# A transformer block on one core: the first LoRA stage run in attention's tiles by the second one's code, with sequence 0's projections dealt into its last rounds

## The chip, the cores and the metric

The kernel runs on one core of a Trainium2 chip. The metric is the device time of one execution in microseconds (us), as the median of several runs of the same build. The core has five engines that take their instructions in order, each from its own stream: TensorE (PE, matmuls and transposes into PSUM), VectorE (DVE), ScalarE (ACT), GpSimd (POOL) and SyncE (SP, which issues the DMAs).

## The reference, cut to what matters

The input `x` has 16 sequences of 512 positions by 256 features, in float32. Six steps follow each other, each added to the residual stream: an FP4-quantised feed-forward, a Mamba mixer, a second pass of the same feed-forward, a LoRA mixture, attention, and the same LoRA mixture again.

```
x = x + 0.5 * ffn(layernorm(x))        # FP4 weights and activations
x = x + mamba(layernorm(x))
x = x + 0.5 * ffn(layernorm(x))        # the same weights
x = x + 0.5 * lora(layernorm(x))       # the first LoRA stage
x = x + attention(layernorm(x))        # 16 heads of 16, ALiBi, causal
x = x + 0.5 * lora(layernorm(x))       # the second LoRA stage, same weights

lora(x):  base   = x @ base_w.T + base_b            # 256 -> 256
          gate   = softmax(x @ router_w.T + router_b).astype(bf16)   # 8 experts
          mid    = x @ lora_A                       # rank 8
          out    = sum_e gate[e] * (mid @ lora_B[e])
          return base + 2 * out
```

## The kernel before, in words

The residual stream stays in SBUF as sixteen tiles `xs[b]`, each with 128 positions on the partitions, 4 chunks and 256 features. `ffn_phase` (L181) runs twice. The last instruction of its second pass on PE is the matmul of L331, and the last Silu of ACT is that of L291.

**The first LoRA stage** is `lora_phase` (L947) with its own pools: two PSUM tiles of two banks under the tag `ob`, two banks under `tr` and two under `o`. It loops over 19 rounds with a pipeline of four steps. In round b it runs `experts(b-3)`, `base(b-2)`, `turn(b-1)` and `norm(b)`. Of each sequence,

- `norm` takes the statistics on DVE (`bn_stats`, `bn_aggr`, L969 and L970), a square root on ACT (L972), a reciprocal and a product on DVE (L974, L976), and the normalised rows on ACT (L981, four instructions);
- `turn` transposes them on PE (L126, eight transposes) and copies them out on ACT (L129, two copies);
- `base` multiplies by the 272 columns of base weight, router and LoRA A (L1001), takes the sums out on DVE (L1005, L1010), and makes the softmax of the gate and the products `cb` with small DVE instructions and an exponential on ACT (L1013 to L1026);
- `experts` transposes `cb` (L1036), copies it on ACT (L1040), multiplies by the stacked LoRA B (L1045) and adds on DVE (L1050).

Between the rounds it draws steps of `constants` (L1102), a generator that loads attention's weights and fills its constants: the query and key tiles on DVE (L1152, L1157), and the `mx` and `va` tiles on POOL (L1185, L1189). In its last three rounds it also normalises and transposes sequence 0 for attention, and runs that sequence's projections by `heads` (L1251) with plain, unpinned matmuls. There the raw queries and keys are parked in the tiles `vas[1:]`, which are filled with ones only afterwards (L1306).

**Attention** is `attn_phase` (L1084). Its pools are opened after `lora_phase` has closed its own: one of SBUF (`a`), and PSUM with two tiles of two banks under `sp`, one under `sw`, and two banks under `mm`. All its PE instructions go through `matmul` and `transpose` (L1199, L1202), which keep them in the order in which the program gives them. So a trace shows them all under L1200 and L1203. `project(b)` (L1205) is a generator: it normalises sequence b (statistics L1214, a logarithm and an exponential on ACT at L1223 and L1224, two Newton steps on DVE, the rows at L1235), transposes it, and multiplies by the query, key and value weights. Each query or key tile leaves by eight DMAs from SP (L1288). `begin(b)` starts it. A unit is one sequence and four heads: `peak_score` and `peak_max` (masked scores and their row maxima, L1346 and L1350) in six steps, then `peak_rows` (L1355, a transpose of the maxima), then `weigh_score`, `weigh_exp`, `apply` and `divide`. The loop over the units (L1697) deals projections and closing work in between by `aside` (L1483).

**The second LoRA stage** has no pools of its own. It borrows attention's: `parts(b)` (L1519) cuts its small tiles out of free query and key tiles (`free`) and of one exponent tile (`rows_of`), and its PSUM tiles are `mm` and `sp`. `mix_norm` (L1533) takes the statistics on DVE, a logarithm and an exponential on ACT (L1545, L1546), then a chain of ten small POOL instructions (L1548 to L1556, two Newton steps and the shift), then the rows on ACT (L1572). `mix_turn`, `mix_base` and `mix_experts` do what `turn`, `base` and `experts` do. `mix_first` handles sequences 0 and 1 beside attention's last units; `mix_rest` the other fourteen, one round each, in an order that is written out:

```
for of in (
    turn, base, base, expert, turn, base, expert, base, expert
):
```

Every instruction that the program does not pin is placed by a scheduler at build time; on the chip each engine then runs its stream in order.

Of the kernel before, what the change touches and what calls it, by code (L numbers as in the profile page):

```python
# [9 lines left out]
F32 = mybir.dt.float32  # L10
BF16 = mybir.dt.bfloat16
# [5 lines left out]
P = 128  # L17
# [19 lines left out]
def macaron_kernel(  # L37
# [83 lines left out]
    def transpose_seq(xh, dst, psum_pool, tag, order=lambda ins: ins):  # L121

        for k in range(KD):
            pt = psum_pool.tile([P, SEQ], F32, name="pt", tag=tag)
            for c in range(NC4):
                order(nc.tensor.transpose(  # L126
                    pt[:, c * P : (c + 1) * P], xh[:, c, k * P : (k + 1) * P], ident
                ))
            nc.scalar.copy(dst[:, k, :], pt)  # L129

# [50 lines left out]
    def ffn_phase(weights, src, dst, prepare=None, raws=(), keep=()):  # L181
        wgT, wuT, wdT = weights
        HF = DFF // 2
        with tc.tile_pool(name="f", bufs=2) as fp, tc.tile_pool(
# [90 lines left out]
            def make_h(b, pair, j):  # L275
# [3 lines left out]
                for half in range(2):  # L279
# [11 lines left out]
                    nc.scalar.activation(sl, g, AF.Silu)  # L291
# [655 lines left out]
    def lora_phase(weights, last, beside=None, heads=None):  # L947


        wx, lb, br = weights  # L950
        W = D + NE + NR
        with tc.tile_pool(name="l", bufs=2) as lp, tc.tile_pool(
            name="l_b", bufs=2, space=PSUM
        ) as ps_b, tc.tile_pool(name="l_ps", bufs=2, space=PSUM) as ps:
            xhs, xTs, copies = {}, {}, []

            cbs = []
            for i in range(3):
                cb = lp.tile([P, NC4, NX], F32, name=f"cb{i}", tag=f"cb{i}", bufs=1)
                nc.gpsimd.memset(cb[:, :, NE * NR :], 1.0)  # L960
                cbs.append(cb)

            def norm(b):

                x = xs[b]
                st = lp.tile([P, NC4, 6], F32, name="st", tag="st")
                mv = lp.tile([P, NC4, 2], F32, name="mv", tag="mv")
                for c in range(NC4):
                    nc.vector.bn_stats(out=st[:, c, :], in_=x[:, c, :])  # L969
                    nc.vector.bn_aggr(out=mv[:, c, :], in_=st[:, c, :])  # L970
                sd = lp.tile([P, NC4], F32, name="sd", tag="sd")
                nc.scalar.activation(sd, mv[:, :, 1], AF.Sqrt, bias=eps)  # L972
                rs = lp.tile([P, NC4], F32, name="rs", tag="rs")
                nc.vector.reciprocal(rs, sd)  # L974
                nm = lp.tile([P, NC4], F32, name="nm", tag="nm")
                nc.vector.scalar_tensor_tensor(  # L976
                    nm, mv[:, :, 0], -1.0, rs, op0=ALU.mult, op1=ALU.mult
                )
                xh = lp.tile([P, NC4, D], F32, name="xh", tag="xh")
                for c in range(NC4):  # L980
                    nc.scalar.activation(  # L981
                        xh[:, c, :], x[:, c, :], AF.Identity,
                        bias=nm[:, c : c + 1], scale=rs[:, c : c + 1],
                    )
                xhs[b] = xh

            def turn(b):
                xT = lp.tile([P, KD, SEQ], F32, name="xT", tag="xT")
                transpose_seq(xhs.pop(b), xT, ps, "tr")
                xTs[b] = xT  # L990

            def base(b):

                xT = xTs.pop(b)
                s = lp.tile([P, NC4, NE + NR], F32, name="s", tag="s")
                for half in range(2):
                    o = ps_b.tile([P, 2, SEQ], F32, name="ob", tag="ob")
                    for j in range(2):
                        c = 2 * half + j
                        for k in range(KD):  # L1000
                            nc.tensor.matmul(  # L1001
                                o[:, j, :W], lhsT=xT[:, k, c * P : (c + 1) * P],
                                rhs=wx[:, k, :], start=(k == 0), stop=(k == KD - 1),
                            )
                    nc.vector.tensor_tensor(  # L1005
                        s[:, 2 * half : 2 * half + 2, :], o[:, :, D:W],
                        br.unsqueeze(1).to_broadcast([P, 2, NE + NR]), op=ALU.add,
                    )
                    xc = xs[b][:, 2 * half : 2 * half + 2, :]
                    nc.vector.tensor_tensor(xc, xc, o[:, :, :D], op=ALU.add)  # L1010
                lg, mid = s[:, :, :NE], s[:, :, NE:]
                mx = lp.tile([P, NC4], F32, name="mx", tag="mx")
                nc.vector.tensor_reduce(mx, lg, axis=AX.X, op=ALU.max)  # L1013
                ex = lp.tile([P, NC4, NE], F32, name="ex", tag="ex")
                nc.vector.tensor_tensor(
                    ex, lg, mx.unsqueeze(2).to_broadcast([P, NC4, NE]), op=ALU.subtract
                )
                nc.scalar.activation(ex, ex, AF.Exp)
                nc.vector.tensor_reduce(mx, ex, axis=AX.X, op=ALU.add)
                nc.vector.reciprocal(mx, mx)  # L1020
                gt = lp.tile([P, NC4, NE], BF16, name="gt", tag="gt")
                nc.vector.tensor_tensor(
                    gt, ex, mx.unsqueeze(2).to_broadcast([P, NC4, NE]), op=ALU.mult
                )
                cb = cbs[b % 3]
                nc.vector.tensor_tensor(  # L1026
                    cb[:, :, : NE * NR].rearrange("p c (e r) -> p c e r", e=NE),
                    gt.unsqueeze(3).to_broadcast([P, NC4, NE, NR]),
                    mid.unsqueeze(2).to_broadcast([P, NC4, NE, NR]), op=ALU.mult,
                )  # L1030

            def experts(b):
                cb = cbs[b % 3]
                pt = ps.tile([P, SEQ], F32, name="ct", tag="tr")
                for c in range(NC4):
                    nc.tensor.transpose(  # L1036
                        pt[:NX, c * P : (c + 1) * P], cb[:, c, :], ident
                    )
                cT = lp.tile([NX, SEQ], F32, name="cT", tag="cT")
                copies.append(nc.scalar.copy(cT, pt[:NX, :]))  # L1040
                for half in range(2):
                    o = ps.tile([P, 2, D], F32, name="o", tag="o")
                    for j in range(2):
                        c = 2 * half + j
                        nc.tensor.matmul(  # L1045
                            o[:, j, :], lhsT=cT[:, c * P : (c + 1) * P], rhs=lb,
                            start=True, stop=True,
                        )
                    xc = xs[b][:, 2 * half : 2 * half + 2, :]
                    nc.vector.tensor_tensor(xc, xc, o, op=ALU.add)  # L1050
                if last:
                    store_x(b)

            for b in range(NB + 3):
                if 0 <= b - 3:
                    experts(b - 3)
                if 0 <= b - 2 < NB:
                    base(b - 2)
                if 0 <= b - 1 < NB:
                    turn(b - 1)  # L1060
                if b < NB:
                    norm(b)
                if heads is not None:
                    if 0 < b < NB:
                        next(beside, None)
                        if b % 2:
                            next(beside, None)
                    if b == NB - 1:
                        for _ in beside:
                            pass  # L1070
                    if b == NB:
                        norm(0)
                    if b == NB + 1:
                        turn(0)
                        first = heads(0, xTs.pop(0), None, ps, "tr", nc.tensor.matmul)
                        for _ in range(4):
                            next(first)
                    if b == NB + 2:
                        for _ in first:
                            pass  # L1080
        return copies[-1]


    def attn_phase(weights):  # L1084
# [17 lines left out]
        def constants(aw):  # L1102
# [79 lines left out]
            for r in range(3):  # L1182
                if r < 2:
                    mx = aw.tile([P, NC4, 4, 32], F32, name=f"mx{r}")
                    nc.gpsimd.memset(mx, 0.0)  # L1185
                    mxs.append(mx)
                va = aw.tile([P, NC4, VW], F32, name=f"va{r}")
                if r == 0:
                    nc.gpsimd.memset(va, 1.0)  # L1189
                vas.append(va)  # L1190
# [14 lines left out]
        def project(b):  # L1205
# [43 lines left out]
            yield from heads(b, xT, ap, ps, "mm", matmul)  # L1249

        def heads(b, xT, ap, ps, tag, matmul):  # L1251


# [609 lines left out]
```

## Time and profile before

| | |
|---|---|
| median of 3 runs | 4329.45 us (4329.03 to 4329.85) |
| the profiled execution | 4323.53 us, its span 4321.8 us |
| mean granted PE clock | 0.976 of full |
| busy share of the span | PE 92%, DVE 86%, ACT 54%, POOL 39% |
| first matmul of the first LoRA stage to its last projection | 2999.92 to 3140.21 us |
| first attention unit's scores begin | 3140.99 us |

The span is what the profiler records of the execution; the execution's own time lies 1.73 us above it, and the median of the plain runs 5.92 us above the profiled one. A busy share is an average over all stages. What a stage is worth is read from the stretch of time in which it runs: which engine is busy there, and what each idle stretch waited for. Times in a trace are counted from the start of the span.

### The profile page before, as it was taken

What the parts mean: (1) busy time and instruction counts of PE and PEld (TensorE: products, weight loads), DVE (VectorE), ACT (ScalarE), POOL (GpSimd) and SP (SyncE); (2) the same over time, 40 slices, a digit from 0 to 9 for tenths busy, and PEclk for the clock granted to TensorE, in tenths of its full rate; (3) what the DMA queues carried; (4) which work ended last, traced back from release to release, by engine and by line L of the source; (5) the groups of instructions that cost most, each with busy time, mean ns of one, the idle gap of its engine ahead of it and who ended that gap; (6) DMA issues with size and microseconds to landing.
All of it is one profiled execution on the core that took longest, in us unless ns stands there. A gap on an engine that the chain in (4) does not pass through costs nothing. (4 is left out here: it accounts for less than half of the span.)

```text
span 4321.8 us, 51496 instructions
## 1 busy us (share of the span) xinstructions
PE 3980.8 (92%) x18786; PEld 2179.5 (50%) x18786; DVE 3735.6 (86%) x4950; ACT 2315.4 (54%) x3478; POOL 1672.8 (39%) x1102
## 2 busy tenths in 40 slices
PE   6999977989888899888888799998999999999999
PEld 4666632333333333333333466666745555555557
DVE  9999838999999999999999899997678778878776
ACT  4444346676767677677666344434624444444434
POOL 3000027888888888888889400000000000000001
PEclk9999999999999999999999999999989999999999
DMA  4000024344444444444442300000010000000002
GB/s 151 15 15 20 15 109 129 119 137 128 127 132 133 141 142 142 142 142 141 142 139 82 114 1 1 1 1 16 2 24 16 18 19 16 18 20 14 20 11 69
DMA packets 120895, 305.16 MB, mean 71 GB/s; under 512 B 25329, under 2 KB 45362, under 8 KB 104002
## 3 DMA queue, kind: packets, MB, share of 16 engines
q1 hardware_dynamic: 120642, 301.88, 22.3%
q8 instruction: 148, 2.42, 0.2%
q14 instruction: 105, 0.86, 0.1%
HBM read 239.68 MB, written 45.35 MB: 66 GB/s over the span
## 5 line engine op out<-in xcount | busy, mean ns | idle before, releaser
L487 POOL TENSOR_TENSOR bx<-dtu,bc 128x1024 f32<-128x1024 f32 x512 | 1193.6, 2359 | 47.5 <-DVE h L883 47.3
L493 PE MATMUL y<-g,ident 128*128 128x512 f32 x2048 | 1007.3, 630 | 130.3 <-DVE g L490 130.1
L883 DVE TENSOR_TENSOR_SCAN h<-da,bx 128x1024 f32<-128x1024 f32 x384 | 879.7, 2291 | 85.4 <-ACT da L484 48.8
L484 ACT ACTIVATE da<-dt,a_neg 128x511 f32<-128x511 f32 x1024 | 703.0, 688 | 217.7 <-DVE hs L883 117.6
L493 PEld LDWEIGHTS y<-g,ident 128*128 128x128 f32 x2048 | 388.3, 198 | 710.0 <-issue 461.9
L1397 ACT ACTIVATE eT<-s 128x768 f32<-128x768 f32 (+1 forms) x384 | 338.6, 882 | 481.0 <-PE s L1200 481.0
L490 DVE TENSOR_TENSOR g<-h,bc 128x1024 f32<-128x1024 f32 x384 | 468.9, 1221 | 28.6 <-DVE h L883 1.4
L1200 PE MATMUL s<-k,q 32*128 32x256 f32 (+3 forms) x2048 | 479.5, 477 | 5.4 <-DVE mx L1350 4.5
L1350 DVE TENSOR_REDUCE mx<-s 128x2 f32<-128x1024 f32 (+3 forms) x512 | 410.3, 823 | 12.4
L1200 PE MATMUL s<-qm,k 32*128 32x512 f32 (+3 forms) x2048 | 387.1, 473 | 8.9 <-ACT eT L1397 7.7
L1600 POOL MEMSET k<- 128x4 f32 x2 | 0.2, 105 | 950.4 <-DVE ku L1282 946.9
L1346 DVE TENSOR_TENSOR s<-s,mask 128x256 f32<-128x256 f32 (+1 forms) x384 | 199.3, 519 | 194.1 <-PE s L1200 191.2
L487 POOL TENSOR_TENSOR g<-hs,bc 128x1024 f32<-128x1024 f32 x128 | 301.3, 2354 | 157.7 <-DVE hs L883 140.4
L291 ACT ACTIVATE sl<-g 128x352 f32<-128x352 f32 x256 | 118.1, 464 | 384.6 <-PE g L286 381.6
L1200 PEld LDWEIGHTS s<-k,q 32*128 32x128 f32 x2048 | 218.6, 186 | 164.1 <-DVE s L1346 80.5
L883 DVE TENSOR_TENSOR_SCAN hs<-da,bx 128x1024 f32<-128x1024 f32 x128 | 291.9, 2281 | 2.5 <-ACT da L484 2.5
L493 PE MATMUL p<-xT,w_in 128*128 128x512 f32 x500 | 242.2, 607 | 19.7 <-ACT xT L484 10.1
L484 ACT ACT_TABLE_LOAD x170 | 218.1, 1283 | 3.0
L960 POOL MEMSET cb<- 128x4 f32 x3 | 0.2, 104 | 561.4 <-PE o L331 561.4
L1200 PEld LDWEIGHTS s<-qm,k 32*128 32x128 f32 x2048 | 170.8, 186 | 58.7 <-ACT eT L1397 42.0
L516 POOL MEMSET xs<- 128x12 f32 x2 | 0.2, 110 | 512.7 <-DMA xd<-x 512.7
L286 PE MATMUL g<-wgT,xT 128*128 128x352 f32 x512 | 182.4, 466 | 0.0
(311 smaller groups left out, 6925.6 us busy)
## 6 DMA issues: line engine op xcount, KB each, us to landing
bc<-bd SPq DMA_DIRECT2D x128, 1024.0 KB, 6.6
xs<-xc SPq DMA_DIRECT2D x240, 256.0 KB, 4.7
xc<-xp SPq DMA_DIRECT2D x60, 256.0 KB, 2.0
x<-_attn_hidden_states_dram SPq DMA_DIRECT2D x16, 512.0 KB, 7.6
xd<-x SPq DMA_DIRECT2D x16, 512.0 KB, 2.6
xo<-xd SPq DMA_DIRECT2D x16, 512.0 KB, 3.6
xe<-xo SPq DMA_DIRECT2D x16, 512.0 KB, 2.6
x<-xe SPq DMA_DIRECT2D x16, 512.0 KB, 10.2
```

What stands on the lines that cost most here:

```text
L286: nc.tensor.matmul(dst, lhsT=xT[:, k, c * P : (c + 1) * P], rhs=w[:, k, f0 : f0 + HF], start=(k == 0), stop=(k == KD - 1),)
L291: nc.scalar.activation(sl, g, AF.Silu)
L484: return tc.keep_in_program_order(nc.scalar.activation(out, in_, func, **kw))
L487: tc.keep_in_program_order(nc.gpsimd.tensor_tensor(out, in0, in1, op=op))
L490: tc.keep_in_program_order(nc.vector.tensor_tensor(out, in0, in1, op=op))
L493: tc.keep_in_program_order(nc.tensor.matmul(out, **kw))
L516: nc.gpsimd.memset(t[:, :, : DCONV - 1], 0.0)
L883: tc.keep_in_program_order(nc.vector.tensor_tensor_scan(flat(h), flat(das[t % 2]), flat(bxs.pop(t)), 0.0, op0=ALU.mult, op1=ALU.add,))
L1200: tc.keep_in_program_order(nc.tensor.matmul(out, **kw))
L1346: nc.vector.tensor_tensor(own, own, const["mask"][:, :w].unsqueeze(1).to_broadcast([P, 2, w]), op=ALU.add)
L1350: nc.vector.tensor_reduce(mx[:, t, 2 * pair : 2 * pair + 2, RM], s[:, :, off : off + (t + 1) * P], axis=AX.X, op=ALU.max,)
L1397: const["exp"] = nc.scalar.activation(eT[:, 2 * pair : 2 * pair + 2, e0 : e0 + w], s[:, :, :w], AF.Exp)
```

## The change

`lora_phase` goes, with its pools, and so does `heads` as a function of its own: its body is again part of `project`. The second stage's functions serve the first stage too. The list `free` stays empty until attention's last sequence, and the functions ask it which stage they are in. While it is empty, all small tiles come from the two exponent tiles in `rows_of`, the rows are normalised on ACT, and nothing is stored. `mix_rest` becomes `mix_rounds(first)`. In the first stage it also draws one step of `constants` per round, begins sequence 0's normalisation in round 16 (of 1 to 19), and lets its projections run from round 17 on: one step of them follows each step of the LoRA work. The rest of them, and `begin(1)`, follow behind. The `va` tiles are all filled with ones by `constants`. The table of logarithm and exponential is loaded on ACT behind the feed-forward's last Silu.

On each engine the streams before and after are the same up to the end of the second feed-forward, except for that table load. They are the same again, in the same order, from early in attention's first units on; on PE the streams differ from the first LoRA transposes up to the last of sequence 0's value projections.

```diff
+    silu = []
...
-                    nc.scalar.activation(sl, g, AF.Silu)
+                    silu.append(nc.scalar.activation(sl, g, AF.Silu))
...
-    def lora_phase(weights, last, beside=None, heads=None):
...
-            for b in range(NB + 3):
-                if 0 <= b - 3:
-                    experts(b - 3)
-                if 0 <= b - 2 < NB:
-                    base(b - 2)
-                if 0 <= b - 1 < NB:
-                    turn(b - 1)
-                if b < NB:
-                    norm(b)
...
                 va = aw.tile([P, NC4, VW], F32, name=f"va{r}")
-                if r == 0:
-                    nc.gpsimd.memset(va, 1.0)
+                nc.gpsimd.memset(va, 1.0)
...
-            yield from heads(b, xT, ap, ps, "mm", matmul)
-
-        def heads(b, xT, ap, ps, tag, matmul):
...
         with tc.tile_pool(name="aw", bufs=1) as aw:
-            behind = lora_phase(weights, False, constants(aw), heads)
...
-                with tc.issue_after(behind.ins):
+                with tc.issue_after(silu[-1].ins):
                     const["exp"] = nc.scalar.preload_act_table_set("natural_log_exp_and_others")
...
-                begin(1)
...
-                free = [t for j in range(NJ) for t in (qs[at(NB - 2, j)], ks[at(NB - 2, j)])]
+                free = []
...
-                    if b % 4 < 2:
+                    if free and b % 4 < 2:
                         four = free[4 * (b % 2) : 4 * (b % 2) + 4]
                     else:
-                        e = rows_of[0].rearrange("p i w -> p (i w)")
+                        e = rows_of[b % 4 // 2].rearrange("p i w -> p (i w)")
...
-                    if b >= 4:
+                    if b >= 4 or not free:
                         nc.gpsimd.tensor_tensor(g, mv[:, :, 0], rs, op=ALU.mult)
                         nc.gpsimd.tensor_scalar(g, g, -1.0, None, op0=ALU.mult)
...
-                        if b < 4:
+                        if b < 4 and free:
                             nc.vector.tensor_scalar(
...
-                    m = 1 if b < 2 else 2
+                    m = 1 if b < 2 and free else 2
...
-                        if half_ == 1:
+                        if half_ == 1 and free:
                             store_x(b)
...
-                def mix_rest():
+                def mix_rounds(first):
-                    for n in range(3, NB + 4):
+                    for n in range(first + 1, NB + 4):
                         none = iter(())
                         turn = mix_turn(n - 1) if n - 1 < NB else none
-                        base = mix_base(n - 2) if 2 <= n - 2 < NB else none
-                        expert = mix_experts(n - 4) if 2 <= n - 4 else none
-                        if 4 <= n < NB:
+                        base = mix_base(n - 2) if first <= n - 2 < NB else none
+                        expert = mix_experts(n - 4) if first <= n - 4 else none
+                        if first + 2 <= n < NB:
                             mix_norm(n)
+                        if not free:
+                            if n < NB:
+                                next(making, None)
+                            if n == NB:
+                                begin(0)
+                                normed = coming.pop(0)
+                            if n == NB + 1:
+                                coming[0] = normed
                         for of in (
                             turn, base, base, expert, turn, base, expert, base, expert
                         ):
...
+                making = constants(aw)
+                for _ in range(2):
+                    rows_of.append(ap.tile([P, 4, EW], F32, name="eT", tag="eT"))
+                mix_norm(0)
+                mix_norm(1)
+                for _ in mix_rounds(0):
+                    next(coming.get(0, none_left), None)
+                for _ in coming.pop(0):
+                    pass
+                started.clear()
+                begin(1)
...
-                        ahead = coming.pop(A[0] + 1, None) or mix_first()
+                        ahead = coming.pop(A[0] + 1, None)
+                        if ahead is None:
+                            for j in range(NJ):
+                                free.extend((qs[at(NB - 2, j)], ks[at(NB - 2, j)]))
+                            ahead = mix_first()
...
-                            rows_of.append(ap.tile([P, 4, EW], F32, name="eT", tag="eT"))
-                            ahead = itertools.chain(ahead, mix_rest())
+                            rows_of[1] = ap.tile([P, 4, EW], F32, name="eT", tag="eT")
+                            ahead = itertools.chain(ahead, mix_rounds(2))
```

More of the change, by code (lines that the diff above doesn't have):

```diff
@@ L945, in lora_weights @@
         return wx, lb, br
-    def lora_phase(weights, last, beside=None, heads=None):
[L950 to L1052, printed above, removed]
-            for b in range(NB + 3):
-                if 0 <= b - 3:
-                    experts(b - 3)
-                if 0 <= b - 2 < NB:
-                    base(b - 2)
-                if 0 <= b - 1 < NB:
-                    turn(b - 1)
-                if b < NB:
-                    norm(b)
[L1063 to L1081, printed above, removed]
@@ L1248, in project @@
                 yield 2, False
-            yield from heads(b, xT, ap, ps, "mm", matmul)
-        def heads(b, xT, ap, ps, tag, matmul):
-            x = xs[b]
-            spare = iter(())
-            if ap is None:
-                spare = iter(
-                    [
-                        va.rearrange("p c w -> p (c w)")[:, i * SEQ : (i + 1) * SEQ]
-                        for va in vas[1:] for i in range(2)
-                    ]
-                )
             bvb, bob, bq_t, bk_t = (const[n] for n in ("bvb", "bob", "bq_t", "bk_t"))
@@ L1265, in heads @@
                 for name, ring in (("q", qs), ("k", ks)):
-                    p = ps.tile([P, SEQ], F32, name="p", tag=tag)
+                    p = ps.tile([P, SEQ], F32, name="p", tag="mm")
                     for k in range(KD):
@@ L1273, in heads @@
                             yield 3, True
-                    r = next(spare, None)
-                    if r is None:
-                        r = ap.tile([P, SEQ], F32, name=f"{name}u", tag=f"{name}u")
+                    r = ap.tile([P, SEQ], F32, name=f"{name}u", tag=f"{name}u")
                     if name == "q":
@@ L1293, in heads @@
             for half in range(2):
-                p = ps.tile([P, 2, D], F32, name="p", tag=tag)
+                p = ps.tile([P, 2, D], F32, name="p", tag="mm")
                 for c in range(2):
@@ L1303, in heads @@
                         yield 3, True
-                if ap is None and half == 0:
-                    for va in vas[1:]:
-                        nc.gpsimd.memset(va, 1.0)
                 dst = vas[b % 3][:, 2 * half : 2 * half + 2, : NH * HV]
@@ L1465, in attn_phase @@
                 pools.update(sbuf=ap, psum=ps)
-                with tc.issue_after(behind.ins):
+                with tc.issue_after(silu[-1].ins):
                     const["exp"] = nc.scalar.preload_act_table_set("natural_log_exp_and_others")
                 units = [(b, j) for b in range(NB) for j in range(NJ)]
-                coming = {}
+                coming, none_left = {}, iter(())
                 def begin(b):
```

## The prediction

> **What bounds the kernel now.** I read the page's slices first: PE is 0.9 busy through attention, but not where the first LoRA stage lies (about 2994 to 3140 us), and the clock row is full nearly everywhere. So I asked for the stretch of that stage and of the step into attention, in windows.
>
> ```profile
> core 0: us, PE busy (x) PEld busy (x) DVE busy (x) ACT busy (x) POOL busy (x), PEclk, DMA share, GB/s
> ...
> 3010.00:3020.00 10.00, 8.06 (x42) 6.10 (x41) 9.67 (x42) 9.80 (x17) 0.00 (x0) 1.00 0.00 0
> ...
> 3100.00:3110.00 10.00, 9.71 (x50) 8.00 (x49) 5.84 (x17) 4.14 (x9) 0.00 (x0) 1.00 0.00 0
> ...
> 3140.00:3150.00 10.00, 2.79 (x15) 1.34 (x15) 9.74 (x36) 0.41 (x2) 1.06 (x1) 0.75 0.21 48
> 3150.00:3160.00 10.00, 10.00 (x25) 4.11 (x25) 6.73 (x21) 1.86 (x3) 1.06 (x1) 0.50 0.05 10
> ```
>
> Early rounds are bound by DVE and ACT (both near 10 of 10), late ones by PE. Then comes a hole: PE has 2.79 of 10 us of work, and behind it the clock is at half. Windows of 2 us show half clock from 3145 until
>
> ```profile
> 3170.00:3172.00 2.00, 2.00 (x10) 0.63 (x4) 0.90 (x3) 0.54 (x1) 0.00 (x0) 0.50 0.25 53
> 3172.00:3174.00 2.00, 2.00 (x8) 0.73 (x10) 0.86 (x1) 0.78 (x2) 0.00 (x0) 0.94 0.02 5
> ```
>
> The timeline names the hole:
>
> ```profile
> 3136.59 3.62 PE L1298 MATMUL p<-wv,xT 128*128 128x256 f32 x16
> ...
> 3140.99 1.14 PE L1200 MATMUL s<-k,q 32*128 32x512 f32 x8 [0.78 <-DVE va L1308]
> ...
> 3148.55 2.30 PE L1203 MATMUL p<-ident,xh 128*128 128x128 f32 x8 [6.42 <-DVE xh L1235]
> ...
> 3167.12 1.11 PE L1203 MATMUL p<-ident,mx 128*128 128x128 f32 x4
> ```
>
> PE waits for sequence 1's normalised rows, because its statistics start on DVE only at 3141.45. The first unit (3140.21 to 3167.12) takes 26.9 us; later ones take about 16 (o matmuls at 3235.34 and 3251.51).
>
> What the second stage's code costs per round, the same trace shows at its end, by ACT's copies of `cT`:
>
> ```profile
> 4247.19 0.58 ACT L1651 COPY q<-p 65x512 f32<-65x512 f32 x1 [1.56 <-PE p L1203]
> ...
> 4253.90 0.58 ACT L1651 COPY q<-p 65x512 f32<-65x512 f32 x1 [1.56 <-PE p L1203]
> ...
> 4260.62 0.58 ACT L1651 COPY eT<-p 65x512 f32<-65x512 f32 x1 [1.56 <-PE p L1203]
> ```
>
> A round is 6.72 us, with PE full (69.85 of 70 us from 4230 to 4300). Rounds of the first stage take 7.9 us: base(1) begins at 3008.79, base(15) at 3119.43, 110.6 over 14.
>
> **The change part by part.** I follow the path from one PE mark to the next. The order of the built streams is taken as given.
>
> *Start, to base(1).* Removed: ACT's square-root tables (the stage has 9 + 9 loads of 1283 ns; one remains, hidden in the feed-forward's tail where ACT is 2.4 of 10 busy). Added: POOL's chain of ten instructions, which in the second stage takes 0.28 us a step (4201.28 to 4204.02, 2.8 us). Ahead of the first chain POOL now has all its fills: `mx` 2 x 0.52 and `va` 3 x 1.06 (rows below), so it is free near 2999.0 and sequence 0's rows start at 3002.05, against 2999.27.
>
> ```profile
> L1189 POOL MEMSET va<- 128x1152 f32 x1 | 1.1, 1057 | 0.0
> L1185 POOL MEMSET mx<- 128x512 f32 x2 | 1.0, 524 | 0.0
> ```
>
> On ACT sequence 1's exponential stands behind sequence 0's four row instructions (2.08), at 3004.1. Its POOL chain, interleaved with sequence 2's (two chains took 3.0 at 4215.1), ends near 3007.8, and its rows near 3010.1. The copy of turn(0)'s second half stands behind them on ACT, so base(0) starts at 3010.7, at half clock (3.93 at full). With turn(1), base(0) and turn(2) behind it, base(1) starts near 3018. That is 9.2 us later than before. Bounds: 5 (clock up at once) to 12 (half clock until 3020).
>
> *Rounds, base(1) to base(15).* PE needs 6.72. DVE's work per round in the first eight, by its starts, is statistics 1.65, base 1.4, softmax 0.9, experts 1.3 and the constants 0.9, so 6.2, in an order where PE waits for it; I take 7.1 for five of them and 6.72 for the seven later rounds. The two fill rounds take 5.5 (no experts yet) and 6.7. Sum 12.2 + 35.5 + 47.0 = 94.7, against 110.6: 15.9 gained. Bounds: 6.72 throughout gives 18; 7.9 in the early five gives 12.
>
> *Tail, base(15) to the last value projection.* Left on PE are one base (3.93), one turn (1.04), three `cT` (0.60), three experts (1.99), queries and keys (2 x 3.71) and values (3.62): 23.8 by busy times. Busy times overlap: a round's 7.56 takes 6.72, so 21.1. New are waits on the two `mm` banks, since each step now lies against the copy-out of a neighbour: three at about 1 to 1.5 us (copy 0.69 or 0.75 and the hand-over, about 0.2 each way) and four of 0.1 to 0.35, together 4.8. So 25.9 against 20.8 (3119.43 to 3140.21): 5.1 lost. Bounds 1 to 9.
>
> So far 9.2 − 15.9 + 5.1 = −1.6: the LoRA stage itself hardly gains, its last projection ending near 3138.6.
>
> *The first unit.* Sequence 1's statistics and rows are now made on DVE within the LoRA rounds, before the first scores. No hole is left, and the clock should stay full. DVE then sets the pace: values and bias 0.69 + 0.68, and six peak steps (mask 0.43 and maximum 1.22 twice, 0.43 and 0.95 twice, 0.70 and 1.02 twice), 10.9; with the hand-overs at both ends 11.4. PE's own work at full clock is near 10.3 (projections of 1.04 each, half of the 2.08 shown at half clock). 11.4 against 26.9: 15.5 gained. SP's queue: the first scores need sixteen of the DMAs, 5.0 us for eight, landing 13 us after the first query tile; PE has 20 us of other work in between, so they are covered by 7.
>
> *The unit's end.* From the maxima's transpose to the next scores, 3167.12 to 3173.60, 6.5 us run at half clock; at full, with the same DVE step of 0.69, 4.6: 1.9 gained.
>
> All else keeps its order, second LoRA stage included. Sum −19.0. Span 4321.8 becomes 4302.8, the profiled time 4323.53 becomes 4304.5, and the median, 5.92 above it, 4310.5.
>
> [...] The row: PE is shown busy without a break from 3150 to 3172 and the clock stays at half for those 22 us, while behind the feed-forward it rose within 6 us of the first transpose. [...] The trace has the duration, so I use it.
>
> [...] The second stage cycles the same two banks, and its granted clock is 1.00 from 4230 to 4300. [...]
>
> **The rivals.**
>
> *Slower: the written PE order makes PE wait in every round.* PE cannot pass a late copy any more, and `mm` has two banks where `tr` and `o` had four. If DVE's constants delay an add each round, two hand-overs (0.58 and 0.69, each with about 0.5 of latency) lie bare: 6.72 + 2.3 = 9.0 a round. Fourteen rounds give 126, 31 more than my sum: 12 slower than before, 4341. It decides above 8.1 us a round (94.7 + 19 over 14). Against: the second stage's full PE. For: DVE there has no constants, and 1.0 us a round idle behind POOL.
>
> *The clock stays low in the first unit although the hole is gone.* The peaks use 32 of 128 rows, and the clock would not rise in 22 us of them. If the short waits of the tail or of the first unit let it fall, 10.3 us of PE work become 20: 10 less gained, 4320. Against: it needed 2.9 us of idle PE before it fell at 3145.0.
>
> *It does not do what it says: a wait takes the hole's place.* If the query and key DMAs land after the values are done, or rows of sequence 1 wait for a late DVE, PE idles again, the clock falls and the first unit keeps its 26.9 and its end 6.5: 17.4 not gained, 4328, no change. For: thirty-two DMAs are 20 us of SP's queue. Against: only the first sixteen matter, with 7 us to spare.
>
> **How the numbers follow.** Forecast 4310.5, chance 0.70; low clock 4320, 0.12; new wait 4328, 0.10; slower 4341, 0.08. About 0.2% (8.7 us) is what a measurement of this kernel can tell from no change. My own bounds: start −4 or +3, rounds ±3, tail ±4, first unit up to 4 longer; taken together about ±6, so 4304 to 4317. The range reaches on over the low clock: 4303 to 4323; left out are most of the new wait and the slower case. Faster: 0.70 and most of the low clock's 0.12 (its 4320 lies at the border), 0.78; same: 0.14; slower: 0.08.
>
> **What would show it.** In the profile after: no table load between the rounds; first transposes near 3002.7; base(1) near 3018 and base(15) near 3113, so copies of `cT` 6.7 to 7.1 apart; last value projection near 3139; transposes of the first maxima 11 to 12 us behind it; windows there with clock 1.00. Copies 8 us apart would prove the slower rival, a wait of some us on a DMA or on `xh` before the first scores the third, and clock 0.50 beside a busy PE the second. I am wrong if the gain comes from the rounds and not from the step into attention.

## The result and the profile after

| | before | after |
|---|---|---|
| median of 6 runs each | 4329.24 us (4324.61 to 4329.85) | 4301.51 us (4299.65 to 4303.09) |
| the profiled execution, its span | 4323.53, 4321.8 us | 4302.86, 4301.1 us |
| ratio of the times | | 0.9939, interval 0.9926 to 0.9952 |

The change gains 0.6%, 27.7 us in the medians. The direction and the mechanism were forecast, the size was not: 4310.5 was predicted, and 4301.5 lies below the range's low end of 4303.

In the windows of the kernel after (the columns are those of the windows shown above: stretch, length, busy time of each engine, granted clock, DMA), the start at half clock is longer than before (17.1 us, up to 3015.3, against 6.8), and the first unit runs at full clock with a busy PE:

```profile
3010.00:3020.00 10.00, 9.68 (x36) 7.19 (x37) 6.86 (x26) 5.63 (x15) 3.48 (x18) 0.74 0.01 2
...
3140.00:3150.00 10.00, 10.00 (x44) 4.05 (x44) 9.09 (x16) 0.69 (x1) 0.00 (x0) 1.00 0.15 34
3150.00:3160.00 10.00, 10.00 (x63) 4.68 (x66) 7.56 (x11) 4.36 (x5) 0.00 (x0) 1.00 0.23 52
```

The timeline of PE shows no hole. Scores follow the values at once, the transposes of sequence 1 follow the scores, and the only wait of the unit is one of 0.98 us for DVE's maxima:

```profile
3136.74 1.14 PE L1065 MATMUL s<-k,q 32*128 32x512 f32 x8
3137.81 1.09 PE L1068 MATMUL p<-ident,xh 128*128 128x128 f32 x8
3139.88 0.59 PE L1065 MATMUL s<-k,q 32*128 32x384 f32 x2 [0.98 <-DVE mx L1196]
...
3148.55 0.66 PE L1068 MATMUL p<-ident,mx 128*128 128x128 f32 x4
```

ACT's copies of `cT` in the first stage now stand 6.7 us apart, as in the second:

```profile
3048.31 0.58 ACT L1495 COPY eT<-p 65x512 f32<-65x512 f32 x1 [1.24 <-PE p L1068]
3055.03 0.58 ACT L1495 COPY eT<-p 65x512 f32<-65x512 f32 x1 [1.45 <-PE p L1068]
```

The feed-forward ended 1.93 us later in this execution than in that of before (2994.99 against 2993.06, the start of its last group of matmuls), with the same code up to there. So the steps are counted from that mark:

| step | before | after | change | predicted |
|---|---|---|---|---|
| feed-forward's last matmuls to base(1) | 15.73 | 23.19 | +7.5 | +9.2 |
| base(1) to base(15) | 110.64 | 95.04 | −15.6 | −15.9 |
| base(15) to the last value projection's end | 20.78 | 23.59 | +2.8 | +5.1 |
| from there to the first maxima's transposes | 26.91 | 11.74 | −15.2 | −15.5 |
| from there to the next scores | 6.48 | 4.49 | −2.0 | −1.9 |
| sum | | | −22.5 | −19.0 |

From those scores to the end the two executions agree within 0.2 us (1148.2 and 1148.1). So the step into attention, the fourth and fifth row, gives 17.2 of the 22.5 us, and the LoRA stage, the first three, gives 5.3, where the prediction had 1.6.

### The profile page after: what moved, and what is told of

Same layout as the page of the kernel before. It is cut to its first block, busy times and chain, and to the rows that moved or that the text cites. A ratio compares the mean times of both kernels' runs of the same rounds, so it can differ in the third digit from the quotient of the medians.

```text
span 4301.1 us, 51611 instructions
## 1 busy us (share of the span) xinstructions
PE 3967.8 (92%) x18786; PEld 2174.3 (51%) x18786; DVE 3733.2 (87%) x4943; ACT 2292.6 (53%) x3473; POOL 1706.4 (40%) x1263
## 5 line engine op out<-in xcount | busy, mean ns | idle before, releaser
L495 PE MATMUL p<-xT,w_in 128*128 128x512 f32 x500 | 242.4, 608 | 19.9 <-ACT xT L486 10.1
L288 PE MATMUL g<-wk,xT 128*128 128x352 f32 x512 | 182.5, 467 | 0.0
```

The source lines that it names most:

```text
L288: nc.tensor.matmul(dst, lhsT=xT[:, k, c * P : (c + 1) * P], rhs=w[:, k, f0 : f0 + HF], start=(k == 0), stop=(k == KD - 1),)
L495: tc.keep_in_program_order(nc.tensor.matmul(out, **kw))
```

## The experiments

Theory A: the gain is the hole and the half clock behind it, paid for a little at the start and in the tail; what is left of the miss comes from half-clock windows that differ from execution to execution. The rivals were that the rounds gained it, that only the idle time counted and not the clock, or that the median stands above a profiled time by a fixed amount.

**The hole put back into the kernel after.** The statistics of sequence 1 wait on DVE for sequence 0's values, as they did before the change:

```diff
+                stats = nc.vector.bn_stats
+                if b == 1:
+                    with tc.issue_after(const["values"].ins):
+                        stats(out=st[:, c, :], in_=x[:, c, :])
+                else:
+                    stats(out=st[:, c, :], in_=x[:, c, :])
...
+                const["values"] = values
```

> The kernel after, with sequence 1's statistics for attention held on DVE until sequence 0's values are out; this puts the hole back and nothing else. Theory A: PE waits 6 to 7 us for the normalised rows, half clock for 20 us and more, first unit 26 to 28 instead of 11.7 and its end 6.5 instead of 4.6: 15 to 18 slower than after, 4317 to 4320, with the scatter of before again if the scatter comes from this spell. Rival (the gain comes from the rounds and the start): at most 3 us slower, 4302 to 4305. Rival (only the hole counts, not the clock): 7 to 8 slower, 4309.

Measured: median 4318.3 over 11 runs (4316.8 to 4321.0), 16.8 above the kernel after. In PE's timeline:

```profile
3131.46 1.14 PE L1065 MATMUL s<-k,q 32*128 32x512 f32 x8
3140.03 2.21 PE L1068 MATMUL p<-ident,xh 128*128 128x128 f32 x8 [7.43 <-DVE xh L1105]
...
3158.52 1.11 PE L1068 MATMUL p<-ident,mx 128*128 128x128 f32 x4
```

PE waits 7.43 us for the rows, the transposes then take twice their time (2.21 us, 1.09 in the kernel after), and the unit (3131.46 to 3158.52) takes 27.1 instead of 11.8 (3136.74 to 3148.55). Its end, up to the next scores at 3166.27, takes 7.8 instead of 4.5. So the prediction's largest terms, 15.5 and 1.9, are shown by putting back their cause alone. The rival in which the rounds gained all of it falls. But the kernel with the hole is still faster than before: by 10.1 in the medians on its own chip (before there 4328.4 over 27 runs), and by 3.2 to 7.6 in the traces (1325.2 us behind the feed-forward, against 1328.4 to 1332.8 further down). That is the LoRA stage's share.

**The hole filled in the kernel before.** Transposes of the identity are put on PE behind the first scores; nothing else moves:

```diff
+                        if u == 0 and n == 1:
+                            p = ps.tile([P, SEQ], F32, name="fill", tag="mm")
+                            for _ in range(46):          # 60 in the second run
+                                transpose(p[:, :P], ident)
```

> The kernel before, with 46 transposes of the identity put on PE behind the first scores (about 6.0 us of dummy work in the hole of 6.4 us); the hole keeps its length, only the clock is kept up. Theory A (half clock behind the hole): clock 1.00 through the first unit, which then takes about 7.9 + 11.4 = 19.3 instead of 26.9, its end 4.6 instead of 6.5; gain 9 to 10 us, about 4319 against 4329, and if before's scatter comes from the spell behind the hole, runs within 2 us of each other. [...] Rival (DVE and not the clock sets the unit): no gain.

Measured: median 4323.1 over 11 runs, with nine of them at 4322 to 4326 and two at 4312.6 and 4313.1. The transposes took 0.114 us each, less than planned, and left 1.25 us idle. In the windows of the profiled execution (one of the nine) the clock falls behind that gap:

```profile
3148.00:3150.00 2.00, 0.76 (x6) 0.34 (x3) 2.00 (x11) 0.00 (x0) 0.00 (x0) 1.00 0.21 49
3150.00:3152.00 2.00, 2.00 (x10) 1.31 (x11) 2.00 (x10) 0.96 (x2) 0.00 (x0) 0.78 0.25 56
3152.00:3154.00 2.00, 2.00 (x5) 0.52 (x4) 2.00 (x10) 0.21 (x1) 0.57 (x1) 0.50 0.10 26
...
3172.00:3174.00 2.00, 2.00 (x5) 0.97 (x4) 1.57 (x2) 1.02 (x1) 0.00 (x0) 0.50 0.12 27
```

It stays at half until 3175 although PE is busy all the time. The other runs have no trace; their mean granted clock is 0.976 to 0.978 in the slower ones and 0.979 and 0.980 in the two faster ones. So the fill was made longer:

> The kernel before with 60 instead of 46 transposes of the identity in the hole: they took 0.114 us each, so 46 left 1.25 us of PE idle, and the clock fell in nine of eleven runs all the same (4322 to 4326), but not in two (4312.6 and 4313.1). With 60 (6.8 us) nothing is left idle. Theory A: clock 1.00 from the hole to the end of the first unit in every run, time near 4313, 12 to 15 below before, the hole's own 6.4 still there. Rival (the work in the fill and in the peaks is too thin to hold the clock): 4322 to 4326 again.

Measured: median 4315.4 over 8 runs, six of them 4313.5 to 4316.1 and two near 4323 with a lower mean clock (0.977 and 0.978 against 0.979 and 0.980), so that the expected full clock "in every run" did not come; before on the same chip 4326.7. The profiled execution has clock 1.00 from 3140 to 3180:

```profile
3140.77 6.77 PE L1203 MATMUL fill<-ident 128*128 128x128 f32 x60
3147.38 1.62 PE L1203 MATMUL p<-ident,xh 128*128 128x128 f32 x8
...
3154.04 0.92 PE L1200 MATMUL s<-k,q 32*128 32x256 f32 x8 [1.24 <-DVE mx L1350]
...
3158.91 0.66 PE L1203 MATMUL p<-ident,mx 128*128 128x128 f32 x4
```

From `xh` to the maxima it takes 11.5 us at full clock against 18.6 at half (3148.55 to 3167.12), and the unit's end 4.5 against 6.5. So the clock alone is worth 7.0 + 2.0 = 9.0 us in the traces, 11.3 in the medians. Most of the remaining 8.1 of the 15.2 is the length of the hole itself: the transposes of the rows begin 8.5 us behind the last value projection here, and 1.0 in the kernel after. Both shares of the term are real; the rival in which only idle time counts falls. The length of a gap alone does not decide: PE waits 1.24 us for DVE's maxima within this unit too, and the clock stays at 1.00.

**The dealing undone.** Sequence 0's projections run in one piece behind the rounds:

```diff
                 for _ in mix_rounds(0):
-                    next(coming.get(0, none_left), None)
+                    pass
```

> The kernel after, with sequence 0's projections run in one piece behind the last LoRA round instead of one step behind each LoRA step. Theory A (the dealing pays by giving the query and key DMAs time): PE's LoRA tail has bare hand-overs but the projections run tightly, so the last value projection ends near 3137 to 3139 as before; but the first query tile is copied out near 3130 instead of 3119.7, its sixteen DMAs take 10 us and land near 3142, so PE waits 4 to 6 us before the first scores, and if its clock falls the first unit takes 18 to 20 instead of 11.7: 5 us slower with the clock up, 12 to 16 slower with it down. Rival (the dealing only fills bare hand-overs, DMAs are covered anyway): 0 to 4 us slower. Rival (the waits on two banks cost more than dealing gives): 1 to 3 us faster.

Measured: 4306.9 over 5 runs, 5.3 above the kernel after, yet base(15) to the end of the last value projection took only 24.3 (23.6 when dealt), and the matmuls did not stand idle for DMAs. The estimate had let the first scores wait for sixteen transfers; the first four heads need only the eight of the queries and, behind them in SP's queue, four of the keys. As time and trace did not fit, the same kernel ran again beside other runs:

> The kernel after with sequence 0's projections run in one piece behind the LoRA rounds, a second time. In its first profile the last value projection ended 24.3 us behind base(15), against 23.6 in the kernel after, the first scores began without the wait on DMAs that was expected, and the feed-forward's last matmul came 1.5 us later than in the kernel after, whose code is the same up to there. Theory A (dealing is worth 0.7 us there, the rest of the 5 us are half-clock windows): time behind the feed-forward within 1 us of 1308.8 again, the feed-forward's end anywhere between 2990 and 2997, the median between 4302 and 4307. Rival (dealing is worth 5 us by something not yet seen): median 4306 to 4307 and 1309 or more behind the feed-forward.

Measured: 4302.3 over 5 runs, 0.8 above the kernel after on the same chip (4301.6). Its timeline of PE and of its weight loads (PEld):

```profile
3131.41 3.62 PE L1065 MATMUL p<-wv,xT 128*128 128x256 f32 x16
3134.96 2.33 PE L1065 MATMUL s<-k,q 32*128 32x512 f32 x8
3135.49 0.29 PEld L1065 LDWEIGHTS s<-k,q 32*128 32x128 f32 x2 [0.24 <-DMA k<-ku]
3136.16 0.29 PEld L1065 LDWEIGHTS s<-k,q 32*128 32x128 f32 x2 [0.38 <-DMA k<-ku]
```

The scores take 2.33 instead of 1.14, because their weight loads wait twice for a key transfer; the first undealt run has the same two waits (0.25 and 0.38). From base(15) to the maxima's transposes it takes 36.1 in both, against 35.3. So dealing is worth 0.8 us in the traces, and 0.8 in the medians is within the scatter of the runs. The other 4.5 of the first reading did not come again; it was taken on another chip, and its cause stays open.

**The kernels again, unchanged.** Three runs ask what an execution differs by.

> The kernel before, unchanged. Its runs so far lie near 4329.5 (four) and near 4324.7 (two), and its profiled one at 4323.5. Theory A: runs differ by how many half-clock spells they have, each a multiple of about 3.4 us at half clock (1.7 us lost), most of them at and behind the hole that starts attention; then both levels come again, 4 to 6 us apart, and the median is between 4324 and 4330. Theory B: the offset of 5.9 us between median and profiled run is one of profiling; then all plain runs lie above the profiled one by 4 to 7 us, here too.

> The kernel after, unchanged. The trace marks, counted from the last matmul of the feed-forward, put the change at 22.5 us between the two first profiled executions, the medians at 27.7. Theory A (runs differ by half-clock windows of 1.7 us each in fixed places; the profiled run of before had few of them, that of after an ordinary number): after's runs scatter by 3 to 6 us around 4301 to 4302, the profiled one anywhere among them, and the steps from the feed-forward's end to the scores of the second unit come again within 0.3 us. Rival (after has a second, slower level that six runs missed): some runs near 4306 to 4310.

> The kernel before, one more look. Behind the feed-forward's last matmul its first profile has 1328.4 us, its second 1332.7. Theory A (the first one was a fortunate draw, ordinary executions have two or three half-clock windows more): 1330 to 1333 again. Rival (the first one was ordinary): 1328 to 1329.

| | runs | span behind the feed-forward's last matmul | half-clock loss from 2480 us to the end |
|---|---|---|---|
| before, first | 4329.2 (6) | 1328.4 | 32.1 |
| before again | 4325.1 (11: 4322.9 to 4330.6) | 1332.8 | 38.5 |
| before, third | one, 4326.4 | 1331.5 | 36.9 |
| after, first | 4301.5 (6) | 1305.8 | 23.4 |
| after again | 4301.6 (5: 4299.5 to 4303.0) | 1308.2 | 26.7 |

The loss is (1 − granted clock) times 2 us, summed over windows of 2 us up to the end of the span. All its spells but the one that the end cuts off are 1.70 us or a multiple of it. They stand at nearly the same few places in every execution (behind the feed-forward, in the hole where there is one, in the second and third unit, in attention's last units and the second LoRA stage; in two of before one more in the first stage's rounds), but how many stand there differs. Where an execution of the same kernel has 3.3 to 6.4 us more of this loss, its span behind the feed-forward is 2.4 to 4.4 longer. So the first profiled execution of before was a fortunate one: to the second unit's scores it took 180.5 us from the feed-forward's last matmuls, the other two 181.4 and 182.8. After took 158.1 and 157.8. The gain by the mean is 23.7, not 22.5. The theory of a fixed distance between profiled time and median falls: the second profiled execution of before (4330.1) lies above its median, and both of after do.

> The kernel after with the hole put back, one more look. In its first profile the feed-forward ended at 2990.4, 2.6 to 4.9 us earlier than in the two of the kernel after, with the same code up to there. Theory A (which half-clock windows fall in the Mamba stage's end is a draw in each execution): the feed-forward ends anywhere between 2990 and 2997, 1325 us remain behind it, within 2.5. Rival (it is a property of the build): 2990.4 again within 0.5.

Measured: 2991.5 for the feed-forward, against 2990.4, and 1325.2 us behind it, as in the first. The time behind it comes again. That its end moved by 1.1 fits the draw of theory A, but both are earlier than all others, so that a share of the build is not excluded.

**The start.** In the kernel after POOL's fills stand ahead of the first chain, and sequence 0's rows ahead of sequence 1's exponential on ACT:

```diff
+                with tc.issue_after(const["chain"].ins):     # a later norm's last POOL step
                     nc.gpsimd.memset(va, 1.0)
...
-                mix_norm(0)
-                mix_norm(1)
+                held = [mix_norm(b, True) for b in range(2)] # both up to the POOL chain
+                for rows in held:                            # then the rows, each of them
+                    rows()                                   # issued after sequence 1's Exp
```

> The kernel after, with POOL's three fills of the value tiles put behind a later normalisation's chain instead of ahead of the first, and on ACT sequence 1's exponential ahead of sequence 0's row instructions. Theory A (the start is set by POOL's fills, by DVE's slow instructions beside them, and by ACT's order): first transposes 1.5 to 2 us earlier, sequence 1's rows 3 us earlier, base(0) near 13.5 us after the feed-forward's last matmul instead of 17.0 and base(1) 3 to 4 us earlier; 2.5 to 4 us faster than after, about 4298. Rival (the later fills stand in the way of the rounds' chains, or the constants on DVE set the early rounds anyway): the gain at base(1) is gone by base(15), 4301.

Measured: 4299.2 over 5 runs (4296.2 to 4300.1), after on the same chip 4301.6. The first transposes come 8.2 us behind the feed-forward's last matmuls instead of 10.0, base(1) 19.9 instead of 23.2, and the values' end keeps the gain (138.4 against 141.8). In the timeline of the kernel after, two of DVE's small instructions run long beside POOL's fill:

```profile
2998.54 2.34 POOL L1054 MEMSET va<- 128x1152 f32 x2
2998.64 1.24 DVE L937 TENSOR_SCALAR lw_x<-lw_x 128x512 f32<-128x512 f32 x1
2999.80 1.10 DVE L1387 TENSOR_SCALAR v<-mv 128x4 f32<-128x4 f32 x1
```

and without the fill they do not:

```profile
2996.24 0.41 DVE L937 TENSOR_SCALAR lw_x<-lw_x 128x512 f32<-128x512 f32 x1
2996.57 0.17 DVE L1388 TENSOR_SCALAR v<-mv 128x4 f32<-128x4 f32 x1
```

The version is faster than both kernels by its median: its ratio to before is 0.9936 (0.9922 to 0.9950), that of after on the same chip 0.9942 (0.9930 to 0.9955). The intervals overlap, so the 2.4 us rest on the steps in the trace more than on the times.

With 73 transposes of the identity on PE between the feed-forward and base(0) besides (50 ahead of the first rows, 3 behind each of the first three transposes, 14 behind the last):

> The kernel after with the reordered start of the earlier run and, besides, 73 transposes of the identity on PE between the feed-forward's last matmul and base(0), 50 of them (5.7 us) ahead of sequence 0's rows, so that the clock does not fall there. Theory A (the start runs on at half clock: both halves of base(0) would be done in 4 us instead of 5.8): no half-clock window from 2993 to 3012, base(1) 1 to 2 us earlier than with the reordered start alone (19.9 us behind the feed-forward's last matmul), about 4297.5. Rival (rows and DVE's constants set the pace there): clock full, base(1) where it was, 4299.

Measured: 4302.0 over 5 runs (4299.6 to 4302.6). The clock is full throughout the start, yet base(1) still begins at 3011.92, 20.0 us behind the feed-forward's last matmuls at 2991.96, because PE now waits for ACT's rows of sequence 2 in front of it. The rival was right that rows set the pace there. That the median lies 2.9 above the reordered start alone was not foreseen: its profile has 8.5 us of half-clock loss from 3168 to 3198 where the other has 5.1, and whether the filling causes that stays open.

## Why the prediction was right or wrong

**Right.** The path was read correctly: the rounds gain, the stage loses part of it again at its start and in its tail, and most of the gain is the step into attention. Rounds, first unit and the unit's end came within 0.4 us of their terms, and the hole's two causes were shown one at a time. The three rivals did not come: rounds of 6.8 us on average instead of 9.0, no wait on transfers or rows, and clock 1.00 through the first unit.

**Wrong: two terms of the sum, and with them "the LoRA stage itself hardly gains".** It gains 5.3, not 1.6. The tail was put at 25.9: 21.1 of work and 4.8 of new waits on the two `mm` banks. It took 23.59, and the records show PE busy for 23.08 of it and idle for 0.51, at two places:

```profile
3116.76 1.12 PE L1065 MATMUL p<-xT,wq 128*128 128x512 f32 x2 [0.24 <-ACT xT L1112]
...
3131.17 1.13 PE L1065 MATMUL p<-wv,xT 128*128 128x256 f32 x4 [0.27 <-DVE ku L1131]
```

So the waits were put 4.3 too high and the work 2.0 too low. Three waits of "about 1 to 1.5 us" were priced as a whole copy-out and two hand-overs, as if nothing of it lay under the neighbouring step's matmuls; that it does lie there is read from the small idle time, and no run takes it apart. The hand-over itself, 0.2 us each way there and 0.5 in the rival of the slow rounds, was an estimate: in the kernel after, a copy of `xT` begins 0.04 us behind the recorded end of its transposes (3116.09 and 3116.13), and the matmul with `wq` above 0.04 behind the end of the copy (3116.72 and 3116.76). The start was put at +9.2 and came at +7.5, 1.7 too dear: base(0) began 17.0 us behind the feed-forward's last matmuls (17.6 predicted), and from there to base(1) it took 6.2 instead of 7.3, the clock being full again from 3015.3. With 0.5 the other way in the other terms this makes 3.5 of the 9.0 us.

**Wrong: the step "the median, 5.92 above it, 4310.5".** This is the larger part of the miss: after's median lies 1.35 below its profiled time, not 5.92 above. The step took one profiled execution and one group of runs as the kernel's own. Over all 65 runs of before its median is 4326.4, which makes 3.1 us of the miss, and its profiled execution had fewer half-clock windows on the changed path than the two others, another 1.2. After's median was the same in both its groups of runs (4301.5 and 4301.6). The remaining 1.2 us stay open, as plain runs leave no trace. That the profiled time itself, 4302.86, came within 1.6 us of its forecast of 4304.5 is luck: the steps were 3.5 short, and the feed-forward happened to end 1.93 later. The range of "about ±6" had bounds for each step and none for this draw of 1.7 us windows; two of them more on either side would have held the result.

**Wrong in an argument.** "It needed 2.9 us of idle PE before it fell" was used against the rival of a low clock. With 1.25 us of idle PE it fell in the profiled execution and, by their times, in eight more of the eleven runs. The rival was nearer than its 0.12 says.

**The clock's return and the two banks.** The prediction took the 22 us at half clock behind the hole as they stand in the trace of before, and that sized the first unit: in the filled kernel PE was again shown busy without a break from 3152 to 3174 at clock 0.50, and the hole put back cost 16.8 us. The spells are of no single length: in the trace of before 27.3 us at half clock in the first unit, 6.8 behind the feed-forward, 3.4 in a round (3048 to 3054). The two `mm` banks did not cost the clock: from 3016 to 3174 the kernel after has no half-clock window, with two `mm` banks in its rounds.

## What to carry to other kernels

An idle stretch of PE can cost its own length and as much again in the half clock behind it: 8 and 9 us here. Look for it at the seam between two phases, where the next phase's first statistics start only when the last phase's results are out, and move that small work ahead of the seam. Before a sum is turned into a time, take two or three profiled executions of the same kernel and count their half-clock windows: one execution can lie 4 us from the next behind the same mark, 2.3 of it on the very path that is changed.

## What the hardware showed unexpectedly

- The clock was easier to keep than to regain. The peaks of 32 rows ran at 1.00 in the kernel after (3140 to 3160, PE 10.00 of 10), and at 0.50 for 24 us with the same kind of PE work behind a gap of 1.25 us. What makes it fall is not the length of the gap alone: behind 1.24 us within the longer filled kernel's first unit it stayed at 1.00.
- In the kernel after the clock falls later all the same, with PE 0.76 of 2 us busy from 3174 to 3176, and is back by 3184: there the fall costs 3.4 us of half clock lost, in the first unit of before 13.7.
- Beside POOL's last two fills of `va` in the kernel after, two of DVE's small instructions took three to six times as long as without them (1.24 against 0.41 us, 1.10 against 0.17), and the last fill lengthened a little itself: 1.34, where the first takes 1.06. DVE's statistics beside the first fill (2997.07 to 2998.13) kept their 0.39. Each of the two slow instructions ends with or just behind a fill (3000.90 against 3000.88, 2999.88 against 2999.60); what couples the two engines there no run shows.
- Identical code ahead of the change ended between 2990.4 and 2996.8 us. The half-clock loss in the Mamba stage's end (2400 to 2480) differed from 8.5 to 13.7 us among these executions, but it does not order them by their ends, so the cause is not settled.
